# Moving two of six adjacency tests per graph from the first SAGE pass to the second

## The chip, the cores and the metric

The kernel runs on one core of a Trainium2 chip. The core has five instruction streams that run side by side[...]: PE (TensorE, the matrix unit), DVE (VectorE), ACT (ScalarE), POOL (GpSimd) and SP (SyncE, which here issues nearly all transfers between HBM and the on-chip memory). Each stream works its own instructions strictly in order. The metric is the time of one execution on the device, in microseconds (us).

## The reference

Sixteen graphs of 1024 nodes with 128 features each go through two layers, each of which ends in a residual sum and a layer norm. Layer 0 is a gated graph network of four steps. Layer 1 thins out the adjacency row by row and then runs three SAGE convolutions with batch norm:

```python
def _sage(x, adj, Wr, Wx, b, mf):
    deg = jnp.clip(jnp.sum(adj, axis=-1, keepdims=True), 1.0, None)
    agg = jnp.einsum('bij,bjd->bid', adj, x) / deg
    out = agg @ Wr + x @ Wx + b
    nrm = jnp.maximum(jnp.linalg.norm(out, axis=-1, keepdims=True), NORM_EPS)
    return out / nrm * mf[..., None]
...
h1 = _bn(jax.nn.relu(_sage(x, adj_d, Wr1, Wx1, b1, mf)), g1, be1)
h2 = _bn(jax.nn.relu(_sage(h1, adj_d, Wr2, Wx2, b2, mf)), g2, be2)
h3 = _bn(jax.nn.relu(_sage(h2, adj_d, Wr3, Wx3, b3, mf)), g3, be3)
xc = jnp.concatenate([h1, h2, h3], axis=-1) * mf[..., None]
return (xc @ Wl + bl) * mf[..., None]
```

The batch norm takes its mean over all nodes of all graphs, so one pass over the sixteen graphs must end before the next can use its scale. This is why there are three passes.

## The kernel before

**Stages.** The first stage runs layer 0 together with the thinning of the adjacency, until about 1284 us. Then come `Sage.first` (first SAGE pass, until about 1746 us), `Sage.second` (until about 1971 us), `Sage.third` and `Sage.last`.

**The tests.** The thinning is done by a fast method that is right only where every entry of the adjacency is 0 or 1 (and the mask as well). The kernel tests this on the side. A graph's adjacency, 1024 x 1024 in fp32, is eight tiles of 128 rows, 512 KB each. `look` (line 2084) is one VectorE instruction over such a tile: it compares each entry with "entry > 0" and adds up the differences into one column of `bad`. It writes an elementwise result that nobody reads, the junk. Tiles 0 and 1 of each graph are tested in the first stage, tiles 2 to 7 in the first SAGE pass: 96 tests. In the third pass `any_bad` takes the maximum over all columns, and a general version of the kernel runs if it isn't zero.

**First pass.** `first` calls `slot(b, t)` for graphs b = -1 to 15 and t = 0 to 15. A slot works on two graphs at once: for graph b ("now") the aggregation and the convolution, for graph n = b + 1 ("nxt") the building of the transposed adjacency `p_at` and its packing to bytes (`pack`), the layer norm and the split of x into a high and a low part (`p_xh`, `p_xl`). The order of instructions on all engines is that of the program, since the schedule is manual. What a slot does for graph b:

- t = 0, 1, 3, 4: aggregation matmuls (L1617) with `p_xh` and `p_xl`, both halves f of the nodes.
- t = 5, 7: `out_first`, the products with the weights, into `p_oa` and `p_ob`.
- t = 6, 8: `scale_rows` (L1417 and L1418, VectorE) gives `s_o`; `squares` (L1425, L1426, ScalarE) gives the row norms `s_ss`.
- t = 7, 9: `rows` (L1446 to L1451, VectorE) gives the output rows `s_r`.
- t = 8, 10: `split_r` makes `p_rh` (L1466, a copy on ScalarE) and `p_rl` (L1467, a subtraction on GpSimd).
- t = 9, 10, 12, 14: the aggregation for the second pass (L1617), with `p_rh` at 9 and 12 and `p_rl` at 10 and 14, written out as `s_ag`.
- t = 11, 13: the rows are transposed (`turn_r`, L1653 and L1654) and written out as `s_rt`.
- t = 2, 5, 8, 10, 12, 14: the tests of tiles 2 to 7 (`check`, which calls `look`), near the end of the slot.

The tiles to be tested are loaded by SP (`load_a`, L1513) into a pool of four buffers, `p_a`; the load of a tile has to wait until the test of the tile four before it has ended. The other transfers of the slot stand in the same SP queue.

**Second pass.** `second` calls `slot_second(b, t)` for b = 0 to 16 and t = 0 to 7. For graph b it does the products with the weights (t = 0 and 3: `out_next`), the row scaling and norms (`chain`, on VectorE and ScalarE, in the same slots), the accumulation of the residual sum into `s_acc` (L1872, VectorE), `rows` (t = 2 and 4) and `split` into `q_rh` and `q_rl` (t = 3 and 5). For the graph before, p, it does the aggregation for the third pass (t = 1, 2, 4, 5, L1861), which reads all of `q_rh` and `q_rl` and the byte adjacency that `unpack` has widened on GpSimd, ScalarE and VectorE (L1812, L1814). `load_second(b + 1)` and `load_bytes` bring in the next graph's data at t = 1, a graph ahead. x, the layer's input, comes into a double-buffered tile `q_x` and is added to the accumulator. A graph moves seven times 512 KB: aggregation in, rows in, x in, two halves of the bytes, and rows and aggregation out.

Before the first and the second pass's results can be used, `weights` runs the batch norm on the statistics that `turn_r` gathered (L1328 and following).

Of the kernel before, what the change touches and what calls it, by code (L numbers as in the profile page):

```python
# [8 lines left out]
F32 = mybir.dt.float32  # L9
BF = mybir.dt.bfloat16  # L10
# [11 lines left out]
P = 128  # L22
B = 16
N = 1024
C = 128
NB = N // P
# [15 lines left out]
def tile_of(b, k):  # L42
    return B // FixPoint.G * NB + b * NB + k
# [874 lines left out]
class Gated:  # L918
# [25 lines left out]
    def bank(self):  # L944
        return self.ps6.tile([P, HF], F32, name="h_g")
# [264 lines left out]
class Sage:  # L1210
# [349 lines left out]
    def check(self, b, k):  # L1560

        if b >= B:
            return
        look(self.nc, self.wk.tile([P, N], BF, name="p_junk", bufs=1), self.bad, self.g[b].pop(("a", k)), b, k)

    def norm_stats(self, b, f):
        nc, g = self.nc, self.g[b]
# [88 lines left out]
    def slot(self, b, t):  # L1656

        nc, g, n = self.nc, self.g.get(b), b + 1
        now, nxt = b >= 0, n < B

        if nxt:
            if t in (4, 6):
                self.load_nr(n + 1, (t - 4) // 2)
            if t == 7:
                self.load_s(n + 1)
            if t in (10, 13):
                self.load_a(n, 2 + t // 13)
        if now and t in (0, 2, 5, 8):
            self.load_a(b, (0, 2, 5, 8).index(t) + 4)

        if now:
            if t in (2, 5):
                g["ag", t // 5] = self.evict(g.pop(("pa", t // 5)), -1, 0)
            if t == 15:
                g["ag2"] = [self.evict(g.pop(("pb", f)), b, f) for f in range(2)]
        if nxt:
            self.unit(n, t)
            if t != 6 or not now:
                self.unit_low(n, t)
            if t:  # L1680
                self.pack(n, t - 1)
        if now and t == 0:
            self.pack(b, 15)
        if now:
            bank = lambda: self.ps3.tile([C, HF], F32, name="p_ag")
            if t in (2, 5):
                self.degrees(b, t // 5)
            if t in (0, 1, 3, 4):
                f, lo = t // 3, t in (1, 4)
                if not lo:  # L1690
                    g["pa", f] = bank()
                self.agg(g["pa", f], (self.xh, self.xl)[lo], g["at"], f, range(NB), not lo, lo)
            if t in (5, 7):
                self.out_first(b, t // 7)
            if t in (6, 8):
                f = t // 8
                g["o", f] = self.scale_rows(b, f, g.pop(("oa", f)), g.pop(("ob", f)))
                if t == 6 and nxt:
                    self.unit_low(n, t)
            if t in (3, 6):  # L1700
                pt = bank() if t == 6 else self.ps1.tile([P, 4, P], F32, name="s_tr").rearrange("p a b -> p (a b)")
                self.degree_columns(b, t // 6, pt[:, :4])
            if t in (7, 9):
                f = t // 9
                g["r", f] = self.rows(b, f, g.pop(("o", f)), g.pop(("ss", f)))
            if t in (8, 10):
                self.split_r(b, t // 10)
            if t in (6, 8):
                g["ss", t // 8] = self.squares(g["o", t // 8])
            if t in (11, 13):  # L1710
                self.turn_r(0, b, t // 13, self.ps1)
            if t in (9, 10, 12, 14):
                part = g["rl"] if t in (10, 14) else g["rh"]
                js = range(4 * (t // 12), 4 * (t // 12) + 4)
                for f in range(2):
                    if t == 9:
                        g["pb", f] = bank()
                    self.agg(g["pb", f], part, g["at"], f, js, t == 9, t == 14)

        if nxt:  # L1720
            if t < 2:
                self.norm_stats(n, t)
            if t in (2, 3):
                self.norm(n, t - 2)
            if t in (6, 8):
                self.turn_x(n, t // 8)
            if t in (7, 12):
                self.split_x(n, t // 12)
        if now and t in (2, 5, 8, 10, 12, 14):
            self.check(b, (2, 5, 8, 10, 12, 14).index(t) + 2)  # L1730

        if now:
            if t == 2:
                nc.sync.dma_start(self.at8[b, 1], g["b", 1])
            if t == 7:
                for i in range(3):
                    nc.sync.dma_start(self.rho[b, i:i + 1, :], g["rho"])
            if t in (13, 15):
                nc.sync.dma_start(self.rt[b, t // 15], g["rt", t // 15])
        if nxt:  # L1740
            if t == 10:
                nc.sync.dma_start(self.at8[n, 0], self.g[n]["b", 0])
            if t == 13:
                nc.sync.dma_start(self.x1[n], self.g[n]["s"])
        if (b, t) == (-1, 11):
            self.load_given()
        if (b, t) == (-1, 15):

            for i in range(3):
                nc.sync.dma_start(self.rho[:, 3 + i, :], self.mask48[:B, :])  # L1750
        if (b, t) == (0, 3):
            self.first_weights()
        if t == 1 and b >= 1:
            for f in range(2):
                nc.sync.dma_start(self.ag[b - 1, f], self.g[b - 1]["ag2"][f])
            del self.g[b - 1]


    def second(self):

        nc, tc = self.nc, self.tc
        with ExitStack() as c:
            pool = lambda name, **k: c.enter_context(tc.tile_pool(name=name, **k))
            self.wk = pool("q_wk", bufs=2)
            self.big = pool("q_at", bufs=2)
            self.ps1 = pool("q_ps1", bufs=1, space=PSUM)
            self.ps2 = pool("q_ps2", bufs=2, space=PSUM)
            c.enter_context(tc.manual_schedule(engines={ET.PE, ET.DVE, ET.Activation, ET.Pool, ET.SP}))
            last, self.g = self.g[B - 1], {}
            self.load_second(0)  # L1770
            self.load_bytes(0, 0)
            for f in range(2):
                nc.sync.dma_start(self.ag[B - 1, f], last["ag2"][f])
            for b in range(B + 1):
                for t in range(8):
                    self.slot_second(b, t)
# [12 lines left out]
    def load_second(self, b):  # L1789
        if b >= B:  # L1790
            return
        nc = self.nc
        self.load_layer(b)
        g = self.g[b]
        g["x"] = self.wk.tile([P, NB, C], F32, name="q_x")
        nc.sync.dma_start(g["x"], self.x1[b])

    def load_bytes(self, b, f):
        if b < B:
# [39 lines left out]
    def slot_second(self, b, t):  # L1839
        nc, g, p = self.nc, self.g.get(b), self.g.get(b - 1)  # L1840
        acc = lambda b, f: self.acc[:, b, 4 * f:4 * f + 4, :]
        if b < B:
            if t == 1:
                self.load_second(b + 1)
                self.load_bytes(b + 1, 0)
            if t == 3:
                self.load_bytes(b, 1)
            if t in (0, 3):
                self.out_next(b, t // 3, self.ps1)
        if p is not None:  # L1850
# [4 lines left out]
            if t in (1, 2, 4, 5):  # L1855
                f = t // 4
# [6 lines left out]
            if t in (3, 6):  # L1863
                f = t // 6
# [3 lines left out]
        if b < B:  # L1868
            if t in (0, 3):
                f = t // 3  # L1870
                pp = self.chain(b, f)
                nc.vector.tensor_add(acc(b, f), pp, g["x"][:, 4 * f:4 * f + 4, :])  # L1872
            if t == 2:
                g["r", 0] = self.rows(b, 0, g.pop(("o", 0)), g.pop(("ss", 0)))
            if t == 3:
                g["rh"] = self.wk.tile([P, NB, C], FR, name="q_rh")
                g["rl"] = self.wk.tile([P, NB, C], FR, name="q_rl")
                self.split(0, g["r", 0], g["rh"], g["rl"])
            if t == 4:
                g["r", 1] = self.rows(b, 1, g.pop(("o", 1)), g.pop(("ss", 1)))  # L1880
                self.turn_r(1, b, 0, self.ps1)
                nc.sync.dma_start(self.rt[b, 0], g["rt", 0])
        if t >= 3:
            if b < B:
                self.unpack(b, t - 3)
        elif p is not None:
            self.unpack(b - 1, t + 5)
# [196 lines left out]
def look(nc, junk, bad, a, b, k):  # L2084

    c = tile_of(b, k)
    nc.vector.scalar_tensor_tensor(junk, a, 0.0, a, op0=ALU.is_gt, op1=ALU.not_equal, accum_out=bad[:, c:c + 1])  # L2087
# [88 lines left out]
```

## Time and profile before

| What | us |
|---|---|
| three runs, median (lowest, highest) | 2167.05 (2165.81, 2168.54) |
| the profiled execution | 2169.4 |
| its span, first to last instruction | 2167.3 |
| DVE busy in the span | 1826.0 |
| ACT busy in the span | 1307.0 |
| POOL busy in the span | 1345.7 |
| the tests of the first pass, 96 of 1.31 on average | 125.7 |
| layer 0 and thinning, from the start to | 1284 |
| first SAGE pass, then to | 1746.7 |
| second SAGE pass, then to | 1971 |
| third pass, head and output, then to | 2167.3 |

The mean granted clock of TensorE is 0.987. The page's section on matmuls warns that they are pipelined and their ends modelled, so a PE that is busy all the time need not be at its peak; what can be read safely are the named waits. The page lists idle time before each group of instructions and what ended it. Idle time of an engine that isn't the bottleneck costs nothing. The windows view gives the busy time of every engine between two moments. A wait is read "who, at which line, waited for whom, at which line".

### The profile page before, as it was taken

The page shows a single profiled execution, that of the slowest core. Times are in us where ns is not written, and L with a number is a line of the kernel's source. Part 1 is how long each engine was busy: PE and PEld are TensorE (multiplying, and loading weights), DVE is VectorE, ACT ScalarE, POOL GpSimd, SP SyncE. Part 2 cuts the span into 40 slices and gives each one's busy share as a digit, 9 for nine tenths or more (in the row PEclk, how much of TensorE's full clock was granted, in tenths as well). Part 3 has the DMA queues.
Part 4 walks back from the last instruction along what each step waited for, and adds up shares of the span by engine and source line. Part 5 has one row for each costly group of instructions (what it writes and reads, how often), then busy time and mean ns, then how long its engine had stood idle before and what let it go on. Part 6 is the DMA issues. An engine that isn't in the chain of part 4 may idle for free. (4 is left out here: it accounts for less than half of the span.)

```text
span 2167.3 us, 33169 instructions
## 1 busy us (share of the span) xinstructions
PE 2065.3 (95%) x10218; PEld 1441.3 (67%) x10219; DVE 1826.0 (84%) x4194; ACT 1307.0 (60%) x3127; POOL 1345.7 (62%) x1451
## 2 busy tenths in 40 slices
PE   7999999999999999999999979999999989999987
PEld 4566556666556665566655657777777768888876
DVE  4898998988998889998989978888888767766887
ACT  3657557565565656656566566666666545555756
POOL 5458558468466476475575456777777535555856
PEclk9999999999999999999999989999999999999999
DMA  8357346456456275464393349888888667775515
GB/s 249 87 119 238 87 121 227 87 145 200 98 156 191 71 209 153 98 203 124 78 268 101 72 169 314 302 305 308 304 306 306 214 239 267 264 265 196 158 40 158
DMA packets 233855, 406.15 MB, mean 187 GB/s; under 512 B 79042, under 2 KB 100196, under 8 KB 233668
## 3 DMA queue, kind: packets, MB, share of 16 engines
q1 hardware_dynamic: 189348, 284.64, 40.5%
q0 software_dynamic: 41616, 117.98, 20.3%
q8 instruction: 83, 1.36, 0.3%
q10 hardware_dynamic: 2704, 1.31, 0.2%
q14 instruction: 104, 0.85, 0.1%
HBM read 313.48 MB, written 109.25 MB: 195 GB/s over the span
## 5 line engine op out<-in xcount | busy, mean ns | idle before, releaser
L1104 PE MATMUL h_g<-h_h,h_wh 128*128 128x512 f32 x768 | 396.1, 597 | 3.9 <-DVE h_r L1116 3.9
L1104 PE MATMUL h_g<-h_ms,h_wi 128*128 128x512 f32 x768 | 392.2, 592 | 0.0
L1123 POOL TENSOR_TENSOR h_zh<-h_r,h_h 128x512 f32<-128x512 f32 x126 | 174.3, 1383 | 256.9 <-ACT h_r L1119 253.7
L737 DVE TENSOR_TENSOR_SCAN f_rank<-f_a,f_first,f_pd 128x1024 f16<-128x1024 bf16 x128 | 299.4, 2345 | 4.2
L1092 PE MATMUL h_g<-h_a,h_hi 128*128 128x512 f32 x1024 | 278.0, 413 | 0.2
L1558 POOL CAST p_b<-p_at 128x512 uint8<-128x512 f32 x256 | 218.7, 875 | 84.0 <-DVE p_at L1550 51.8
L1104 PEld LDWEIGHTS h_g<-h_ms,h_wi 128*128 128x128 f32 x768 | 145.5, 190 | 184.4 <-issue 167.9
L1092 PE MATMUL h_g<-h_a,h_lo 128*128 128x512 f32 x1024 | 262.1, 393 | 0.3 <-DVE h_lo L1030 0.3
L1092 PEld LDWEIGHTS h_g<-h_a,h_hi 128*128 128x128 f32 x1024 | 190.1, 188 | 60.0 <-issue 21.5
L1092 PEld LDWEIGHTS h_g<-h_a,h_lo 128*128 128x128 f32 x1024 | 189.7, 188 | 39.3 <-DVE h_lo L1030 1.2
L1104 PEld LDWEIGHTS h_g<-h_h,h_wh 128*128 128x128 f32 x768 | 133.3, 190 | 101.2 <-issue 72.8
L1125 POOL TENSOR_TENSOR h_h<-h_h,h_zh 128x512 f32<-128x512 f32 x126 | 179.9, 1428 | 9.9
L1119 ACT ACTIVATE h_r<-h_r,h_bi 128x512 f32<-128x512 f32 x128 | 92.4, 722 | 151.5 <-DVE h_r L1118 151.5
L1124 POOL TENSOR_TENSOR h_zh<-h_z,h_zh 128x512 f32<-128x512 f32 x126 | 162.1, 1286 | 9.9
L1095 ACT COPY h_ms<-h_g 128x512 f32<-128x512 f32 x128 | 73.7, 576 | 149.2 <-PE h_g L1092 149.2
L1425 ACT ACTIVATE s_junk<-s_o 128x128 bf16<-128x128 f32 x256 | 76.1, 298 | 142.8 <-DVE s_o L1418 131.9
L910 ACT ACTIVATE f_u<-f_rank,f_q 128x128 f16<-128x128 f16 (+7 forms) x128 | 110.5, 867 | 69.8 <-DVE f_rank L850 68.8
L2087 DVE SCALAR_TENSOR_TENSOR p_junk<-p_a 128x1024 bf16<-128x1024 f32 x96 | 125.7, 1309 | 0.0
L778 POOL TENSOR_SCALAR_AFFINE_SELECT f_both<-f_both 128x512 bf16<-128x512 bf16 x32 | 20.4, 639 | 164.3 <-DVE f_both L777 164.2
L1825 PE MATMUL q_ob<-s_wxp,q_xt 128*128 128x256 f32 x512 | 122.1, 382 | 0.0
L1550 DVE SCALAR_TENSOR_TENSOR p_at<-p_nr,p_u 128x128 fp32r<-128x128 bf16 (+1 forms) x192 | 102.6, 543 | 19.5 <-ACT p_at L1542 13.5
L887 ACT ACTIVATE f_pd<-f_rank,f_q 128x128 f32<-128x128 f16 x128 | 59.1, 462 | 98.3 <-DVE f_q L701 95.1
(306 smaller groups left out, 4918.3 us busy)
## 6 DMA issues: line engine op xcount, KB each, us to landing
h_a<-in_adj_dram POOLq DMA_DIRECT2D x128, 512.0 KB, 9.4
p_a<-in_adj_dram SPq DMA_DIRECT2D x96, 512.0 KB
f_a<-in_adj_dram POOLq DMA_DIRECT2D x128, 256.0 KB, 6.3
e_nr<-f_nr SPq DMA_DIRECT2D x128, 256.0 KB
p_nr<-e_nr SPq DMA_DIRECT2D x32, 1024.0 KB
s_at<-p_b SPq DMA_DIRECT2D x32, 512.0 KB
s_ag<-s_ag SPq DMA_DIRECT2D x64, 256.0 KB
q_agi<-s_ag SPq DMA_DIRECT2D x32, 512.0 KB
```

Of the source, the lines that this page charges most:

```text
L737: nc.vector.tensor_tensor_scan(out, a, other[:, 0, 0:1].to_broadcast([P, N]), start, op0=ALU.add, op1=ALU.bypass)
L910: nc.scalar.activation(u[:, :n1], rank[:, g, :n1], AF.Abs, bias=q[:, 1, g:g + 1], scale=q[:, 0, g:g + 1])
L1092: nc.tensor.matmul(pm[f], part[:, j, :], st.adj[j][:, half[f]], start=(j == 0 and n == 0), stop=(j == NB - 1 and n == 1))
L1104: nc.tensor.matmul(pg, lhs, rhs, start=(i == 0), stop=(i == len(mm) - 1))
L1119: nc.scalar.activation(r, r, AF.Tanh, bias=bias(self.bi, 2))
L1123: aid.tensor_tensor(d, r, h, ALU.subtract)
L1124: aid.tensor_tensor(d, z, d, ALU.mult)
L1125: aid.tensor_tensor(h, h, d, ALU.add)
L1550: self.nc.vector.scalar_tensor_tensor(g["at"][:, j, c0:c0 + low], v[:, j, c0:c0 + low], 0.0, pu[:, :low], op0=ALU.is_lt, op1=ALU.is_lt)
L1558: self.nc.gpsimd.tensor_copy(g["b", f][:, j, :], g["at"][:, j, f * HF:(f + 1) * HF].bitcast(F32))
L1825: nc.tensor.matmul(pb[:, i], g["xt"][:, f, blk], self.wxp, start=(i % 2 == 0), stop=False)
L2087: nc.vector.scalar_tensor_tensor(junk, a, 0.0, a, op0=ALU.is_gt, op1=ALU.not_equal, accum_out=bad[:, c:c + 1])
```

## The change

Two of the six tests per graph leave the first pass. Graphs 1 to 14 test tiles 2 to 5 there, at slots 2, 10, 12 and 14; tiles 6 and 7 are loaded and tested in the second pass. Graph 0 keeps all six tests in the first pass (at the same slots as before, in another order of tiles). Graph 15 keeps five, at slots 2, 4, 6, 8 and 10. In all, 67 tests stay and 29 move.

In the second pass the tiles come into a new pool of two buffers, `q_a`. Tile 6 of graph b + 1 is loaded at t = 4 of graph b and tested at t = 3 of graph b + 1, just after the accumulation. Tile 7 of graph b is loaded at t = 1 of graph b and tested at t = 0 of the graph after it, also after the accumulation.

Room for that pool comes from `q_x`: x is now loaded by SP straight into its place in `s_acc`, and the accumulation adds to what is there. The junk of a test in these passes is no longer written to a tile of its own (`p_junk`); it goes into the first half of the tile that is being tested, as bf16.

```diff
@@ check
-        look(self.nc, self.wk.tile([P, N], BF, name="p_junk", bufs=1), self.bad, self.g[b].pop(("a", k)), b, k)
+        a = self.g[b].pop(("a", k))
+        look(self.nc, a.bitcast(BF)[:, :N], self.bad, a, b, k)
@@ slot
-            if t in (10, 13):
-                self.load_a(n, 2 + t // 13)
-        if now and t in (0, 2, 5, 8):
-            self.load_a(b, (0, 2, 5, 8).index(t) + 4)
+            if t == 10:
+                self.load_a(n, 2)
+            if t == 13 and n == B - 1:
+                self.load_a(n, 3)
+        loads = {2: 3, 5: 4, 8: 5}
+        if b == 0:
+            loads = {0: 6, 1: 7, **loads}
+        if b == B - 1:
+            loads = {0: 4, 2: 5, 4: 7}
+        if now and t in loads:
+            self.load_a(b, loads[t])
...
-        if now and t in (2, 5, 8, 10, 12, 14):
-            self.check(b, (2, 5, 8, 10, 12, 14).index(t) + 2)
+        tests = {2: 2, 10: 3, 12: 4, 14: 5}
+        if b == 0:
+            tests = {5: 6, 8: 7, **tests}
+        if b == B - 1:
+            tests = {2: 2, 4: 3, 6: 4, 8: 5, 10: 7}
+        if now and t in tests:
+            self.check(b, tests[t])
@@ second
+            self.ap = pool("q_a", bufs=2)
@@ load_second
-        g["x"] = self.wk.tile([P, NB, C], F32, name="q_x")
-        nc.sync.dma_start(g["x"], self.x1[b])
+        nc.sync.dma_start(self.acc[:, b], self.x1[b])
@@ slot_second
                 self.load_bytes(b + 1, 0)
+                if 0 < b < B - 1:
+                    self.load_a(b, 7)
...
-                nc.vector.tensor_add(acc(b, f), pp, g["x"][:, 4 * f:4 * f + 4, :])
+                nc.vector.tensor_add(acc(b, f), pp, acc(b, f))
+                if t == 3 and b:
+                    self.check(b, 6)
+                elif t == 0 and b > 1:
+                    self.check(b - 1, 7)
...
                 nc.sync.dma_start(self.rt[b, 0], g["rt", 0])
+                self.load_a(b + 1, 6)
```

## The prediction

> **What bounds the kernel now.** I read the busy table of the page first and then cut the span into its passes with the windows view; an average over the span mixes passes with different limits.
>
> ```profile
> core 0: us, PE busy (x) PEld busy (x) DVE busy (x) ACT busy (x) POOL busy (x), PEclk, DMA share, GB/s
> ...
> 1314.00:1706.00 392.00, 365.92 (x2720) 296.67 (x2719) 347.08 (x877) 255.89 (x729) 286.94 (x283) 1.00 0.87 300
> ...
> 1774.00:1971.00 197.00, 196.12 (x1121) 167.42 (x1120) 140.03 (x255) 113.98 (x368) 105.97 (x87) 1.00 0.75 254
> ```
>
> The first row is the steady part of the first SAGE pass, the second that of the second pass. In the first pass PE is idle for 26.1 of 392 us; in the second for 0.9 of 197. The change takes VectorE work out of the pass in which PE has holes and puts it into the one in which PE has none. A graph takes 27.6 us in the first pass (starts of the same matmul group at 1565.75, 1593.31 and 1620.87 in the timeline) and 14.0 us in the second (1836.31, 1850.31, 1864.28).
>
> What ends PE's holes in the first pass, from the waits between 1330 and 1720 us (who waited for whom: total us, times, longest):
>
> ```profile
> PE p_ag L1617 <- POOL p_rl L1467: 11.5, 14, 0.8
> PE p_ag L1617 <- ACT p_rh L1466: 11.1, 14, 1.1
> PE s_tr L1472 <- ACT p_xt L1595: 3.0, 14, 0.3
> ```
>
> Each comes once per graph: 0.82 + 0.79 + 0.21 = 1.8 us, all of PE's idle time in a graph. Behind them stands VectorE, as the timeline of one graph shows (start, us, engine, line, operation):
>
> ```profile
> 1503.91 1.21 DVE L2087 SCALAR_TENSOR_TENSOR p_junk<-p_a 128x1024 bf16<-128x1024 f32 x1
> ...
> 1505.06 0.67 DVE L1417 TENSOR_TENSOR s_o<-p_oa,s_rdeg 128x512 f32<-128x512 f32 x1
> ...
> 1506.56 0.31 ACT L1425 ACTIVATE s_junk<-s_o 128x128 bf16<-128x128 f32 x1 [2.59 <-DVE s_o L1418]
> ...
> 1510.24 2.12 PE L1617 MATMUL p_ag<-p_at,p_rh 128*128 128x512 f32 x8 [0.76 <-ACT p_rh L1466]
> ...
> 1510.80 1.45 DVE L2087 SCALAR_TENSOR_TENSOR p_junk<-p_a 128x1024 bf16<-128x1024 f32 x1
> ...
> 1511.13 2.24 POOL L1467 TENSOR_TENSOR p_rl<-s_r,p_rh 128x512 fp32r<-128x512 f32 x1
> ...
> 1513.42 2.12 PE L1617 MATMUL p_ag<-p_at,p_rl 128*128 128x512 f32 x8 [0.82 <-POOL p_rl L1467]
> ```
>
> The reader is to see two tests (L2087), those of slots 5 and 8. The first holds up s_o, on which ScalarE's squares have waited 2.59 us. The second runs beside p_rl on GpSimd, which takes 2.24 us here; the same 128x512 subtraction takes 1.29 us in the second pass (q_rl, median). PE waits for both results. These two tests are the ones that leave.
>
> For the second pass, the waits between 1770 and 1970 us say where VectorE has room:
>
> ```profile
> DVE s_st L1654 <- ACT s_rt L1653: 34.5, 14, 2.7
> DVE s_ss L1446 <- ACT s_ss L1426: 14.8, 15, 1.0
> ```
>
> **What the Trainium skill says.** "Perfetto Trace Analysis", Identifying the Most-Contended Engine: matmul busy time is no measure of distance to the roofline, weight-load busy time is better. It agrees here: PEld is 76% of the first window and 85% of the second, so I count PE's named waits, not its busy share. "GPSIMD Engine Reference", Key points: GpSimd shares its SBUF interfaces with VectorE and contends with VectorE instructions that have two SBUF inputs. The test is one (it reads its tile twice), and 2.24 against 1.29 us agrees. "DMA: Bandwidth & Descriptors", Where 436 GB/s comes from: a ceiling of 435 GB/s for the fabric and some 358 for a core's HBM share when both cores of a pair stream. Here 254 GB/s at share 0.75 means 339 at a full one, and pure loads reached 419 (window 1751 to 1754). "VectorE: DVE Perf Modes", Why `tensor_tensor` can't do 2×_2P or 4×: with fp32 and two tensors, one element per cycle, so an estimated 1.07 us for 1024 elements; the trace has 1.20 at least, 1.31 on average in the steady pass. Where the junk result goes (now into the tile tested) should not matter: 0 per test; a loss of 0.1 us on 96 tests would be 10 us of VectorE, mostly under other engines' work.
>
> **First pass, graphs 1 to 14: what goes.** Two tests per graph and their two 512 KB loads. I follow the graph above; PE's slot 5 starts at 1502.54 in either case.
> - s_o's multiply needs p_oa (PE done 1503.88) and VectorE (done with L1603 at 1503.99): it starts at 1504.0 instead of 1505.06. Its add needs p_ob, done 1505.05: ends 1505.8 instead of 1506.52. Gain 0.7.
> - Squares, root and p_xt copy move 0.7 earlier (p_xt done 1507.8 instead of 1508.55), so the 0.19 wait of the transposes at 1508.60 goes. Row scaling (L1451) ends 1508.8 instead of 1509.48.
> - What is late next for p_rh is ScalarE's own order: the copy L1542 of slot 8 needs p_u from PE (1508.02 plus 0.39), so it ends about 1509.05, p_rh about 1509.65, and PE starts at 1509.7 instead of 1510.24. Gain 0.54; some 0.4 of idle time stays.
> - p_rl: GpSimd gets p_xl's input 0.7 earlier, then packs (0.60), and starts p_rl at about 1510.4 with no test beside it: 1.29 us, done 1511.7. PE, after 2.12 us of p_rh matmuls and 0.4 of transposes, wants it at about 1512.05. The whole 0.82 goes.
>
> Sum 0.54 + 0.82 = 1.36 us per graph. Later slots follow: the second half's p_rh would be ready at 1513.8 against a need at 1514.9. Bounds: 0.6 (only one of the two waits goes) to 1.8 (no idle left). I take 1.36, 14 graphs: 19.0 us (8.4 to 25). SP only gains here: it spends 196.6 us waiting for the p_junk tests before its loads (51 waits of L1513); with four loads per graph in four buffers each finds its buffer free. Graph 0 keeps six tests: 0, with tile 6 loaded five slots ahead of its test, where DMA has no backlog.
>
> **Graph 15 and the end of the pass.** There PE waits along one chain. The tests of slots 5, 12 and 14 go, those of slots 4 and 6 come. Slot 4's fits the 1.98 us before L1603 at 1723.20. Without slot 5's, s_o's add ends at 1725.3 instead of 1726.15, and the PE wait of 0.73 on s_o goes; the chain moves 0.75 up. At the end, batch_norm (L1328, 1740.52) starts straight after slot 14's test; without it and the 0.75, at 1738.7. Taken: 1.8 us; 0 if a transfer or PE's last matmuls end there instead, 2.5 at most.
>
> **Second pass: what comes.** 29 tests, 29 loads.
> - VectorE: 9.8 us busy in a graph of 14.0, plus 2 x 1.2 to 1.83 (the longest test of the trace): 12.2 to 13.5. The test of slot 0 follows the accumulation (1861.25 to 1861.93) and has 2.65 us until the next L1654 at 1864.59: hidden even when stretched. The test of slot 3 lies in the 0.99 us before L1446: 0.3 to 0.9 late. Behind it are row scaling, q_rh on ScalarE and q_rl on GpSimd (1860.81 to 1862.11); PE wants the second half of q_rl about 1863.5. Cover 1.4 us: cost 0. If it is gone, each us costs a us per graph.
> - GpSimd beside the slot-0 test: its two casts (2.03 us from 1862.05) may take 3.3; their halves are wanted from 1868. Hidden.
> - DMA: 3.67 MB per graph become 4.72. At 339 GB/s that is 13.9 of 14.0 us; counting the new loads at the 400 or so of pure loads, 10.8 + 2.6 = 13.4. Loads are issued 9 to 12 us ahead of use, so a queue that is nearly full only takes slack. Cost 0 to 10, taken 1.
> - SP: two issues of 0.4 us more per graph. Tile 7's load waits for the slot-0 test of the graph before (till 1863.3); behind it is the store of rt, which waits for ScalarE until 1864.58 anyway. Tile 6's stands after the other rt store, its buffer long free. Cost 0.
> - x straight into the accumulator: same bytes; the add reads the tile it writes, one instruction as before; the load no longer waits for an earlier add. Cost 0, within 0.1 us per add either way.
>
> **Sum.** The profiled execution took 2169.4 us (span 2167.3), 0.1% above the median of 2167.05. 2169.4 - 19.0 - 1.8 + 1.0 = 2149.6; on the median's footing 2147.3.
>
> **Rivals.**
> - Half the gain (22%): the order of ScalarE and GpSimd keeps p_rh and p_rl late, or a new wait opens in slots 10 to 14. 0.6 us per graph, 8.4 + 0.5 - 1 = 8: about 2159. For it: those engines work in order and are 65 and 73% busy. Against: both waits repeat with the same length beside the same tests.
> - Slower (9%): the DMA queue of the second pass fills. The point is where 14 graphs give back the 20.8 us: 15.5 us per graph, 4.72 MB at 305 GB/s. Should writes mixed with these loads sustain only 285 GB/s, a graph takes 16.6 us, 36 us more: about 2182. For it: share 0.75 with 29% more bytes. Against: 300 GB/s at share 0.87 in the first pass.
> - No change (5%): VectorE's slot-3 test makes q_rl late by 1.4 us per graph, 20 us: 2167.
> - The likeliest (64%): 2147, own range 2141 to 2155.
>
> What can be told from no change is about 0.2%, 4 us. Faster takes the likeliest and the half gain: 0.86; same 0.05; slower 0.09. Range 2140 to 2162: the bounds of the first pass (25 + 2.5 us gained; 8 gained less 3 in the second).
>
> **What would show it.** First pass: period 26.2 us; PE's wait for p_rl gone, that for p_rh near 0.4; p_rl near 1.3 us in its first half. Second pass: period 14.0, PE without waits, VectorE near 88%, DMA share 0.95. Wrong if the second-pass period grows, PE waits there for q_rl, q_at or a transfer, or the first-pass period stays above 27.

## The result: 28 us faster

The kernel after takes 2139.76 us (median of 4 runs, 2138.47 to 2140.92) against 2167.8 us for the kernel before in the same session (2165.81 to 2170.38): ratio 0.987, 95% interval 0.9853 to 0.9887. The forecast was 2147.0 with a range from 2140 to 2162. The direction and the place of the gain were right; the size was not: 28 us where 20 were predicted, and the time lies 0.24 us below the range's low end.

The windows view of the profile after, for the steady part of the first SAGE pass and for the second pass (columns as in the prediction's first fence):

```profile
core 0: us, PE busy (x) PEld busy (x) DVE busy (x) ACT busy (x) POOL busy (x), PEclk, DMA share, GB/s
1313.00:1680.00 367.00, 357.89 (x2705) 294.33 (x2703) 307.17 (x820) 253.28 (x722) 257.66 (x283) 1.00 0.78 284
...
1746.00:1940.00 194.00, 194.00 (x1112) 166.29 (x1112) 168.05 (x308) 111.35 (x364) 117.33 (x84) 1.00 0.95 328
```

In the first pass VectorE's share falls from 89% (347.08 of 392) to 84%, PE's idle share from 6.7% to 2.5%. In the second pass VectorE rises from 71 to 87% and the DMA share from 0.75 to 0.95, and PE still has no gap. A graph of the first pass now takes 25.92 us against 27.68 (mean of 13 periods between slot 6's transposes of x on PE), one of the second pass 13.97, as before.

Of PE's three waits per graph in the first pass one is left in the view of waits (1330 to 1690 us: who waited for whom, total us, times, longest):

```profile
PE p_ag L1618 <- ACT p_rh L1466: 7.3, 14, 0.5
```

The timeline of one graph after, at the place that the prediction showed of before (start, us, engine, line, operation, idle time before it):

```profile
1517.81 0.69 DVE L1417 TENSOR_TENSOR s_o<-p_oa,s_rdeg 128x512 f32<-128x512 f32 x1
...
1519.10 0.64 PE L1472 MATMUL s_tr<-ident,p_s 128*128 128x128 f32 x4
...
1519.70 0.31 ACT L1425 ACTIVATE s_junk<-s_o 128x128 bf16<-128x128 f32 x1 [1.85 <-DVE s_o L1418]
...
1522.34 0.60 ACT L1542 ACTIVATE p_at<-p_u 128x512 fp32r<-128x512 f32 x1
...
1522.83 0.61 ACT L1466 CAST p_rh<-s_r 128x512 fp32r<-128x512 f32 x1
...
1523.49 1.70 PEld L1618 LDWEIGHTS p_ag<-p_at,p_rh 128*128 128x128 f32 x8 [0.70 <-ACT p_rh L1466]
1523.49 2.14 PE L1618 MATMUL p_ag<-p_at,p_rh 128*128 128x512 f32 x8 [0.53 <-ACT p_rh L1466]
...
1524.28 1.29 POOL L1467 TENSOR_TENSOR p_rl<-s_r,p_rh 128x512 fp32r<-128x512 f32 x1
...
1525.47 0.40 PE L1537 MATMUL p_u<-ident_b,p_nr 128*128 128x128 bf16 x4
1525.68 2.08 PE L1618 MATMUL p_ag<-p_at,p_rl 128*128 128x512 f32 x8
```

With no test ahead of it, s_o no longer starts late, and the squares have waited 1.85 us instead of 2.59. With no test beside it, p_rl takes 1.29 us instead of 2.24 and is done at 1525.57, before PE asks for it. What is left is the wait for p_rh, 0.53 us in the line of the matmuls and 0.70 in that of their weight loads (PEld).

Where the 28 us come from, by the same instructions in both traces:

| stretch | predicted | measured |
|---|---|---|
| graphs 1 to 14 of the first pass | 19.0 | 14 x (27.68 - 25.92) = 24.6 |
| up to graph 1 | 0 | 1.3 (1338.95 to 1337.66) |
| graph 15 and end of the pass | 1.8 | 1.9 |
| second pass | -1.0 | 0 |

The sum is 27.8. (The two profiled executions differ by more, 30.9 us; the one of before was among the slower of its runs and the one of after the fastest of four. The rest lies behind the second pass: from the third pass's first sum to the end, 181.5 us before and 178.8 after. It is no gain of the change, since the run with more loads below has the same code there as the kernel after and takes 181.3.)

### The profile page after: what moved, and what is told of

It reads as the page before. It is cut to its first block, busy times and chain, and to the rows that moved or that the text cites. A ratio compares the mean times of both kernels' runs of the same rounds, so it can differ in the third digit from the quotient of the medians.

```text
span 2136.5 us, 33076 instructions
## 1 busy us (share of the span) xinstructions
PE 2052.7 (96%) x10219; PEld 1435.3 (67%) x10219; DVE 1814.3 (85%) x4194; ACT 1305.9 (61%) x3127; POOL 1333.8 (62%) x1451
## 3 DMA queue, kind: packets, MB, share of 16 engines
q8 instruction: 83, 1.36, 0.3%
## 5 line engine op out<-in xcount | busy, mean ns | idle before, releaser
L1558 POOL CAST p_b<-p_at 128x512 uint8<-128x512 f32 x256 | 203.7, 817 | 86.9 <-DVE p_at L1550 48.5
L2107 DVE SCALAR_TENSOR_TENSOR p_a<-p_a 128x1024 bf16<-128x1024 f32 x96 | 126.3, 1315 | 0.0
L1550 DVE SCALAR_TENSOR_TENSOR p_at<-p_nr,p_u 128x128 fp32r<-128x128 bf16 (+1 forms) x192 | 102.6, 541 | 16.5 <-ACT p_at L1542 10.0
```

The source lines that it names most:

```text
L1558: self.nc.gpsimd.tensor_copy(g["b", f][:, j, :], g["at"][:, j, f * HF:(f + 1) * HF].bitcast(F32))
```

## The experiments

Three theories were set against each other. *Place*: a test costs what it delays on the way to PE's two holes, at p_rh and at p_rl. *Amount*: the pass got less VectorE work, and where it stood doesn't matter. *Transfer*: two 512 KB loads fewer, and an SP queue that no longer waits for tests. Each kernel was compared with the kernel before on its own chip. The median of before there was 2169.75 us for the runs without slot 5's, slot 8's and both tests and for the one with two loads fewer; 2168.64 for those without the tests of slots 12 and 14, with all tests off slots 5 and 8, with the split of r first and with shared squares; and 2167.74 for the other four. "rh" is the time from slot 6's transposes of x to the first matmul that reads p_rh, "rl" from there to the first that reads p_rl, each a mean over the 13 steady graphs (12 in the run without slot 8's test): before 5.14 and 3.18 us, after 4.39 and 2.17.

**One test left out, then both.** The edit without slot 5's; the two others have (8,) and (5, 8) in its place.

```diff
         if now and t in (2, 5, 8, 10, 12, 14):
-            self.check(b, (2, 5, 8, 10, 12, 14).index(t) + 2)
+            if 0 < b < B - 1 and t in (5,):
+                g.pop(("a", (2, 5, 8, 10, 12, 14).index(t) + 2))
+            else:
+                self.check(b, (2, 5, 8, 10, 12, 14).index(t) + 2)
```

> The kernel before, in which graphs 1 to 14 leave out the VectorE test of slot 5 (tile 4); all six loads stay, and the result column of an untested tile stays zero. Place theory (a test costs what it delays on the way to PE's two holes): the part of the gain that lies at p_rh and at the x transposes ahead of it goes, 0.6 to 0.75 us per graph, 8 to 10.5 us in all, and PE's hole at p_rl keeps its 1.0 us. Amount theory (less VectorE work in the pass, wherever it stood): one test of 1.31 us in 14 graphs, half of the 24.6 us of the first pass, about 12. Transfer theory (two loads fewer, and SP no longer held up by tests): the loads are all there, 0 us.

> The kernel before, in which graphs 1 to 14 leave out the test of slot 8 (tile 5); all six loads stay, untested columns stay zero. Place theory: p_rl on GpSimd, with no two-input VectorE instruction beside it, takes 1.3 us instead of 2.2 and PE's hole at p_rl goes whole: 0.9 to 1.0 us per graph, 12.5 to 14 us; the wait for p_rh stays at 0.79. Amount theory: the same as without the slot-5 test, about 12. Transfer theory: 0.

> The kernel before, in which graphs 1 to 14 leave out the tests of slots 5 and 8 (tiles 4 and 5); all six loads stay, untested columns stay zero. Place theory and amount theory: the whole gain of the first pass in these graphs, 1.76 us per graph, 24 to 25 us. Transfer theory: 0, with the gain still to come from the loads.

| left out | time | ratio (95%) | rh | rl |
|---|---|---|---|---|
| slot 5 | 2158.01 | 0.994 (0.9922 to 0.9958) | 4.39 | 3.10 |
| slot 8 | 2158.36 | 0.9941 (0.9925 to 0.9958) | 5.22 | 2.23 |
| both | 2143.05 | 0.9877 (0.9859 to 0.9895) | 4.39 | 2.17 |

The waits of the run without slot 5's test, and then of the one without slot 8's (same window):

```profile
PE p_ag L1617 <- POOL p_rl L1467: 9.5, 13, 0.8
...
PE p_ag L1617 <- ACT p_rh L1466: 6.9, 13, 0.6
```

```profile
PE p_ag L1617 <- ACT p_rh L1466: 10.0, 13, 0.8
...
PE s_tr L1472 <- ACT p_xt L1595: 3.2, 13, 0.3
```

The reader is to see that each test owns one hole. Without slot 5's the wait for p_xt is gone and that for p_rh falls, while p_rl is waited for as before; without slot 8's it is p_rl that is gone. The times alone don't separate place from amount, since 11.7 and 11.4 us lie near both. Of the transfer theory the loads are out: the whole gain comes with all of them in place (26.7 us, interval 22.8 to 30.6). Its other half, the SP queue, is not: SP's waits for the first pass's tests fall from 204.1 to 64.7 us in the run without both (1300 to 1740 us). The next run separates that.

**Two loads fewer, six tests kept.**

```diff
-            if t in (10, 13):
-                self.load_a(n, 2 + t // 13)
-        if now and t in (0, 2, 5, 8):
-            self.load_a(b, (0, 2, 5, 8).index(t) + 4)
+            if t == 10:
+                self.load_a(n, 2)
...
+        loads = {2: 3, 5: 4, 8: 5} if 0 < b < B - 1 else {0: 4, 2: 5, 5: 6, 8: 7}
...
+        tests = dict(zip((2, 5, 8, 10, 12, 14), (2, 2, 3, 3, 4, 5) if 0 < b < B - 1 else range(2, 8)))
...
```

> The kernel before, in which graphs 1 to 14 load only tiles 2 to 5 (issued in slot 10 of the graph before and in slots 2, 5 and 8), and six tests still stand in slots 2, 5, 8, 10, 12 and 14: those of tiles 2 and 3 are done twice, tiles 6 and 7 are not tested and their columns stay zero. Place theory and amount theory: the same tests in the same slots, so 0 us, within 2. Transfer theory (two 512 KB loads fewer per graph, SP's queue freer): most of the 28 us. Both together: something in between.

2166.82 us, ratio 0.9983 (0.9977 to 0.999), rh 5.04, rl 3.18: 2.9 us, and no hole closed, although SP's waits for tests fell further, to 10.2 us. So neither the loads nor SP's queue held PE in the first pass of the kernel before.

**The same amount taken away elsewhere.** Slots 12 and 14 in place of slots 5 and 8:

```diff
+            if 0 < b < B - 1 and t in (12, 14):
```

> The kernel before, in which graphs 1 to 14 leave out the tests of slots 12 and 14 (tiles 6 and 7) instead; all six loads stay, untested columns stay zero. Place theory: nothing that PE waits for stands behind these two tests, and those of slots 5 and 8 remain: 0 us, within 3, with rh still 5.1 us after slot 6's transposes and rl 3.2 us after rh. Amount theory (the same 2.6 us less VectorE work per graph): 24 to 27 us faster, as without the tests of slots 5 and 8. Transfer theory: 0.

2166.38 us, ratio 0.9989 (0.9982 to 0.9996), rh 5.06, rl 3.18. As much VectorE work less as in the run without slots 5 and 8, and 2.3 us instead of 26.7. That ends the amount theory.

**The small edits alone** (junk into the tile tested, x into the accumulator).

```diff
+        a = self.g[b].pop(("a", k))
+        look(self.nc, a.bitcast(BF)[:, :N], self.bad, a, b, k)
...
+        nc.sync.dma_start(self.acc[:, b], self.x1[b])
```

> The kernel before with only the two small edits of the change: the junk result of each test goes into the tile tested, and x is loaded straight into the accumulator. All theories: 0 us, within 2; a test keeps its 1.31 us. If the in-place result cost 0.1 us per test, 3 to 8 us slower.

2165.91 us, ratio 0.9989 (0.998 to 0.9997), rh 5.11, rl 3.18. Three quite different edits that leave the holes alone (this one and the two ahead of it) all came out 1.8 to 2.9 us below before. What they have in common was not found, so no part of that size is put down to an edit. (In the kernel before 6 of the 13 graphs have an rh of 5.1 to 5.4, the others 5.03 or 5.04. In the two runs ahead of this one a single graph is still above 5.04, and by their periods that makes 0.8 and 1.5 us. Whether the edits did it was not tested.)

**All six tests kept in the first pass, off slots 5 and 8.**

```diff
+            if t in (12, 13, 14):
+                self.load_a(n, t - 10)
+        loads = {0: 5, 3: 6, 11: 7}
...
+        tests = {2: 2, 10: 3, 11: 4, 12: 5, 13: 6, 14: 7}
```

> The kernel before with all six tests still in the first pass, but in slots 2, 10, 11, 12, 13 and 14, with the loads in slots 12, 13, 14, 0, 3 and 11 to fit four buffers. Place theory: most of the gain comes without the second pass: 15 to 25 us, rh at 4.4 us and rl at 2.2 us as in the kernel after; what is missing would be a new wait in slots 11 to 15, where VectorE then does five tests in a row. Amount theory: VectorE's work per graph is the same, 0 us. Transfer theory: the same bytes, 0 us.

2259.51 us, ratio 1.0417 (1.0399 to 1.0434): a clear miss, 91 us slower. The two holes did shrink as the place theory says (rh 4.39 and rl 2.16, as in the kernel after), but the period rose to 33.5 us (mean of 12). Its waits, of ScalarE and PE and then of SP's own queue:

```profile
ACT s_ag L1623 <- DMA s_ag<-s_ag: 44.8, 11, 4.9
...
PE s_tr L1610 <- ACT p_row L1604: 36.9, 11, 4.2
...
PE p_u L1537 <- DVE p_at L1550: 24.2, 21, 2.1
```

```profile
SPq L1513 <- DVE p_junk L2089: 141.1, 30, 8.8
```

Two chains of waits are new. The first runs through SP, which worked in order here. Slot 0's load needs the buffer of the tile that is tested in slot 14; with five tests in a row that test ran at 1529.16 to 1530.38 in one graph, and only then could SP issue the load (1530.58) and the stores of ag behind it (1531.07). Two s_ag buffers wait for those stores, ScalarE waits 4.83 us for a buffer until 1538.89, and PE waits for ScalarE. So a test can also cost through the queue that waits for its buffer. Not all of the wait is the queue's, though: the data of the stores were ready at 1528.15, so the queue held them for 2.9 us, and the rest went by until they had landed, with 387 GB/s moving from 1530 to 1534. The sum of SP's waits for tests says nothing by itself: in the kernel before it is larger (196.6 us in the prediction's window), and the run with two loads fewer shows that it held up nothing there. The second chain is VectorE's own: p_at (L1550) stands between the five tests in its order, and PE waits for it 24.2 us in the window, some 2 per graph. A schedule of this kind with the loads behind the stores wasn't tried.

**How much room the second pass has.** First more VectorE work, then more transfers, both on the kernel after.

```diff
                 if t == 3 and b:
+                    a = g["a", 6]
+                    self.check(b, 6)
+                    g["a", 6] = a
                     self.check(b, 6)
```

> The kernel after, with the second pass's slot-3 test (tile 6) done twice in each of 15 graphs, 1.2 us more VectorE work ahead of L1446. By the trace of after, q_rl's second half is done 1.8 us ahead of the matmuls that read it, and VectorE has 12.2 of 14.0 us busy: hidden, 0 to 4 us. If the cover at q_rl is gone sooner (VectorE's and GpSimd's work beside each other lengthens too), up to 1.2 us per graph, 17 us slower than the kernel after, and a PE wait on q_rl.

2174.91 us, ratio to before 1.0036 (1.0022 to 1.0051): some 35 us slower than the kernel after. Both expectations were too low. A graph takes 16.21 us instead of 13.97 (mean of 12 periods, 1759.03 to 1953.57), so 1.22 us of test cost 2.2. The timeline of one graph shows why:

```profile
1856.33 1.22 DVE L2110 SCALAR_TENSOR_TENSOR p_a<-p_a 128x1024 bf16<-128x1024 f32 x1
...
1856.69 1.99 POOL L1467 TENSOR_TENSOR q_rl<-s_r,q_rh 128x512 fp32r<-128x512 f32 x1 [6.41 <-ACT q_rh L1466]
...
1857.48 1.23 DVE L1446 TENSOR_SCALAR s_ss<-s_ss 128x4 f32<-128x4 f32 x1
...
1861.33 1.08 PE L1472 MATMUL s_tr<-ident,s_r 128*128 128x128 f32 x4 [2.06 <-DVE s_r L1451]
```

GpSimd's q_rl starts at 1856.69 beside the second test and takes 1.99 us instead of 1.29, as though it got going only when that test ended at 1857.5. VectorE's next step, a 128x4 operation that takes 0.15 us elsewhere in this pass, then takes 1.23 and ends with q_rl; the steps after it are stretched beside GpSimd's casts too. s_r ends at 1861.1, and PE, which wanted it at 1859.3, waits. In the kernel after, the single test ends before q_rl starts (1841.73 and 1842.14 in one graph). Beside q_rl only the row scaling (L1451) is stretched there, to 1.65 us, and PE waits for nothing. So the slot-3 test is free at this place, but there is no room for another behind it.

```diff
                 self.load_a(b + 1, 6)
+                self.load_more(b + 1, 6)
...
+    def load_more(self, b, k):
+        if b < B:
+            t = self.ap.tile([P, 896], F32, name="q_more", bufs=1)
+            self.nc.sync.dma_start(t, self.adj[b, k * P:(k + 1) * P, :896])
```

> The kernel after, with 448 KB more loaded (and not read) beside each of the two 512 KB adjacency loads in a graph of the second pass: about 5.6 MB per graph instead of 4.7. If 328 GB/s at share 0.95 is nearly all that these transfers can do, a graph takes 5.6 MB at 345 GB/s or 16.3 us instead of 14.0, about 30 us slower than the kernel after, with PE waiting for loads. If pure loads run at 400 GB/s and more beside the rest, 15 us or less: under 15 us slower.

2143.14 us (0.988, 0.9864 to 0.9897): some 3 us above the kernel after, not 30. The window of its second pass:

```profile
1746.00:1940.00 194.00, 194.00 (x1113) 166.41 (x1112) 168.04 (x307) 111.65 (x361) 117.94 (x84) 1.00 1.02 396
```

The queues carry 396 GB/s at share 1.02, the graph still takes 13.97 us (starts at 1747.81, 1761.79, 1775.78), and PE has no gap. The share isn't a measure of what is left here: 328 GB/s at 0.95 had at least 68 GB/s to spare.

**Towards a better version.** In the kernel after PE still waits for p_rh. Three orders were tried, each on top of the one before: the split of r's first half ahead of slot 8's other ScalarE and GpSimd work; two of the four squares of slot 6 on VectorE; the split of x's first half in slot 11 instead of 7.

```diff
+        if now and t == 8:
+            self.split_r(b, 0)
         if nxt:
             self.unit(n, t)
...
+                if t == 6:
+                    g["ss", 0] = self.shared_squares(g["o", 0])
                 if t == 6 and nxt:
                     self.unit_low(n, t)
...
-            if t in (7, 12):
+            if t in (11, 12):
                 self.split_x(n, t // 12)
```

> The kernel after, with one order changed: in slot 8 the split of r's first half (p_rh on ScalarE, p_rl on GpSimd) is issued ahead of that slot's relu copy on ScalarE and of the byte cast on GpSimd. By the chain read in the trace of after, p_rh then waits only for s_r: it starts 0.2 us earlier, PE's hole at p_rh of 0.7 us per graph becomes 0.5, 3 us faster than the kernel after in 15 graphs (about 2137). If ScalarE's copy or the byte cast was needed sooner, 0 or slower.

> The kernel after, with the order of the run before and, in slot 6, two of the four squares of s_o on VectorE instead of ScalarE (issued ahead of that slot's low half of p_at). The root is then ready some 0.45 us earlier and with it s_r, p_rh and PE: the hole at p_rh goes but for 0.1 us, 0.6 per graph, 9 us faster than the kernel after (about 2131). If VectorE's two squares (some 0.6 us) make p_at or s_rdeg late, a new wait of PE in slots 7 to 9 and less than 3 us.

> The kernel of the run with shared squares, with one more order changed: the split of x's first half (p_xh on ScalarE, p_xl on GpSimd) is issued in slot 11 instead of 7. If p_xl on GpSimd is what held VectorE's small multiply with the mask (1.08 instead of 0.17 us) and so s_r, p_rh and PE, rh falls from 5.55 us after slot 6's transposes to 4.3 to 4.6, and the time from 2156 to 2135 to 2142. If the shared squares themselves are the loss, rh stays near 5.5 and the time near 2156.

| kernel | time | ratio to before (95%) | rh | rl |
|---|---|---|---|---|
| split of r first | 2137.89 | 0.9856 (0.9839 to 0.9872) | 4.29 | 2.17 |
| and shared squares | 2156.14 | 0.9941 (0.9924 to 0.9957) | 5.55 | 2.16 |
| and split of x later | 2141.26 | 0.9879 (0.9862 to 0.9895) | 4.64 | 2.17 |

The first gains 0.1 us of rh per graph where 0.2 was expected; its interval overlaps that of the kernel after, so it beats before for certain and after only perhaps. The second is a miss. Its timeline:

```profile
1531.28 1.26 POOL L1467 TENSOR_TENSOR p_xl<-p_s,p_xh 128x508 fp32r<-128x508 f32 x1 [0.30 <-ACT p_xh L1466]
...
1531.49 1.08 DVE L1448 TENSOR_TENSOR s_ss<-s_ss,mask 128x4 f32<-128x4 f32 x1
```

The shorter ScalarE part let p_xl start earlier, just ahead of VectorE's multiply with the mask, which takes 0.17 us otherwise and here ends with p_xl (1532.57 and 1532.54). With p_xl moved away rh falls by 0.9 us, which confirms it; but it stays 0.35 us above that of the run with only the split of r first. VectorE's order makes that up: its two squares stand ahead of p_at and s_rdeg, so L1446 starts 2.49 us after slot 6's transposes instead of 2.16, although the root it needs is ready earlier. So the shared squares bring nothing.

## Why the prediction was right or wrong

**Right: what goes and where.** The tests of slots 5 and 8 held PE at p_rh and at p_rl. Each of the two runs with one test left out closes its own hole, the two together give the first pass's gain, and the same amount of work taken out of slots 12 and 14 gives nothing of it. The chain was followed correctly too: s_o's add ends with p_ob, p_rl takes 1.29 us, and what stays is p_rh.

**Wrong: the size of "0.54 + 0.82 = 1.36 us per graph".** Measured 1.76: 0.75 at p_rh and 1.01 at p_rl. Both terms were mis-sized, for three reasons that make up the missing 0.40.

*p_rl, 1.01 instead of 0.82.* The step that failed is the first one, "0.82 + 0.79 + 0.21 = 1.8 us, all of PE's idle time in a graph". It took named waits for the size of the holes, as the part ahead of the prediction also says that named waits can be read safely. A named wait of a matmul runs from the end that the record gives to the group ahead of it, and those ends are drawn too late. The group ahead of p_rl in the trace of before, and PE's weight loads at its three waits:

```profile
1508.60 0.42 PEld L1472 LDWEIGHTS s_tr<-ident,p_s 128*128 128x128 f32 x4 [0.36 <-ACT p_xt L1595]
...
1510.24 1.69 PEld L1617 LDWEIGHTS p_ag<-p_at,p_rh 128*128 128x128 f32 x8 [0.94 <-ACT p_rh L1466]
...
1512.21 0.40 PE L1537 MATMUL p_u<-ident_b,p_nr 128*128 128x128 bf16 x4
...
1513.42 1.69 PEld L1617 LDWEIGHTS p_ag<-p_at,p_rl 128*128 128x128 f32 x8 [0.99 <-POOL p_rl L1467]
```

Drawn, the group ends at 1512.61, and the wait to 1513.42 is 0.82. But in the graph after that was shown above, the same group starts at 1525.47 and the next one at 1525.68: it holds PE for 0.21 us, not 0.40. The hole of before was 1513.42 - 1512.21 - 0.21 = 1.00. The weight loads say the same: they waited 0.36, 0.94 and 0.99 us where the matmuls' lines have 0.19, 0.76 and 0.82, so some 0.18 is missing from each. On the mean of the graphs PE's holes were 1.82 + 3 x 0.18 = 2.4 us, and the one that stays is 0.53 + 0.18 = 0.7: 1.7 is gone, by this reading of the trace. The prediction's upper bound, 1.8 with "no idle left", had the wrong reason: 1.76 is gone and 0.7 is left. The Trainium skill says it ("Perfetto Trace Analysis", Tensor Engine Instruction: a matmul's end is estimated, its profile time "a model, not a measurement"), and the trace agrees with 0.40 drawn against 0.21 taken.

*p_rh, 0.75 instead of 0.54.* Here the prediction followed starts, and 0.10 was lost by adding drawn lengths on ScalarE: "it ends about 1509.05, p_rh about 1509.65, and PE starts at 1509.7". In the kernel after the copy L1542 starts at 1522.34 and is drawn 0.60 us, and p_rh starts at 1522.83, 0.11 before that end. PE starts 4.39 us after slot 6's transposes; in the graph that the prediction followed, where these start at 1505.21, that is 1509.60. The other 0.11 is the choice of this graph: its rh is 5.03, one of the shortest, and the mean is 5.14.

**Graph 0: predicted 0, measured 1.3.** Not shown to be a gain. The same marker of graph 1 stands between 1335.05 and 1339.81 in the runs without slots 5 and 8 and with two loads fewer, which change nothing in graph 0.

**Graph 15: predicted 1.8, measured 1.9.** Right in sum, in part by luck. The two steps that were named came about as forecast: s_o's chain gained 0.83 us (0.75 said) and the batch norm after the last test 1.02 (1.05 left for it). But three things that were not named moved as well and nearly cancelled. PE's eight matmuls with p_rh took 3.44 us before (1729.87 to 1733.31), at a granted clock of 0.53, and 1.95 after (1703.92 to 1705.87), at 1.00: a gain of 1.49. PE lost 0.71 at p_row, since ScalarE waited 4.41 us there for an s_ag buffer whose store landed late. And 0.43 was lost between the batch norm and the second pass's first products.

**Second pass: predicted +1 (0 to 10), measured 0.** The rival with the slower ending was priced at 285 to 305 GB/s; 396 GB/s were sustained in the same pass with no PE wait, so what it feared does not hold here, and the upper bound of 10 was too high. The prediction read "254 GB/s at share 0.75 means 339 at a full one"; the run with more loads had 396 at 1.02, so the share did not give the limit. The other rival, VectorE's slot-3 test making q_rl late, had its place nearly right: another 1.2 us there costs 2.2 per graph, but through s_r, before q_rl is wanted.

**The half gain (22%)** did not come: no new wait opened in slots 10 to 14.

## What to carry to other kernels

A piece of work off the critical engine costs what stands behind it, not what it takes: the same 2.6 us per graph was worth 26.7 us in two slots and at most 2.3 in two others. Before a hole of PE is priced from a named wait, measure start to start on PE and subtract what the group ahead takes when nothing holds it, or read the wait in the line of the weight loads, and do it for more than one graph. And when VectorE work is moved, look at what GpSimd starts beside it, and at what SP has queued behind the buffer that it frees.

## What the runs showed of the hardware

- Some instructions of VectorE and GpSimd exclude each other here rather than share. p_rl of 1.29 us takes 2.24 when a test that began earlier still has 1.05 to run (until its accumulator is read at 1512.18); in the first pass its median falls from 1898 to 1426 ns when slot 8's test leaves, and stays at 1895 when those of slots 12 and 14 leave. The other way round a 128x4 operation of VectorE takes 1.08 or 1.23 us instead of 0.17 or 0.15 and ends with GpSimd's instruction. The Trainium skill describes it as an exclusive lock held for the whole instruction ("SBUF — State Buffer", SBUF: two separate sides), and these numbers agree. It is not so for every pair: in the kernel after q_rl (1832.31, 1.29 us) runs beside s_o's add (1832.33, 0.69) and the accumulation (1832.93, 0.68), which each read one operand from PSUM, and none of the three is stretched. The prediction used only that the two contend.
- 396 GB/s of mixed loads and stores at a DMA share of 1.02, with PE never waiting (the run with more loads; one core running).
- A test whose result goes into the tile that it reads costs the same: 1310 ns on average over 96 in the same slots (the run with the small edits alone), against 1309 before.
